# Transforms in two tiles, their products issued in two groups, and k moved ahead of the taps, in a two-layer convolution kernel

## The chip, the cores and the metric

The kernel runs on one core of a Trainium2 chip. A core has five engines with queues of their own: TensorE (PE) for matrix products, VectorE (DVE) and ScalarE (ACT) for elementwise work, GpSimd (POOL), and SyncE (SP), which here issues all transfers. An engine works its queue in order; between engines, instructions wait on semaphores. TensorE reads SBUF and writes PSUM, the accumulator memory; VectorE and ScalarE read both. The metric is the device time of one launch in microseconds (us). Before the change three timed runs gave 3358.13, 3359.34 and 3363.5 us, median 3359.34.

## The reference

x is (4, 64, 256, 256) in float32. Two layers, each with a residual:

```
x = x + L0(gn(x));  x = x + L1(gn(x))        # gn: group norm, 32 groups of 2 channels
L0: h = gelu(conv3x3(x, c1));  h = c2 * h    # 1x1, 64 -> 128 channels
    xa, k = split(h)
    xs = gelu(vertical3(horizontal3(xa)))    # depthwise
    gate = top 2 of 3 of softmax(mean(xs) @ gate_w)
    out = xs + sum_i gate_i * w3_i((w2_i k) * (w1_i xs));  L0 = proj * out
L1: h = relu(bn(conv3x3(x, quantized w1)));  relu(bn(conv3x3(h, quantized w2)) + x)
```

Batch norm (bn) needs statistics over all four images, so layer 1 is cut into two passes and a last elementwise pass.

## The kernel before, in words

**Stages.** First comes layer 0 for the images b = 0 to 3, called the front here (about 57 to 1530 us of the profiled execution), interleaved with the statistics of the next image and with the second half of layer 0 (the expert output, `plan_out`) of the image before. Then come the first convolution of layer 1, its second convolution, and the last pass, which TensorE has no part in. The change touches the front alone.

**The front.** An image is worked in 32 octets (n = 0 to 31) of 8 rows, one per step; step g = 32 b + n. The 3x3 convolution uses a transform along the row: for every pair of neighbouring pixels POOL forms four combinations of the inputs, the products 0 to 3 (`front_v`, L479 to L487), and TensorE multiplies each with a weight of its own. The weights of products 0 and 3 are `c1s`, those of 1 and 2 are `u12`, with a factor 0.5 in them (L419). All combinations lie in one SBUF tile, `v_ring`, with 12 slots, that is three octets of 4 slots each. One call of `front_v` makes half an octet: 4 POOL instructions of 128x256 elements, products 1, 2, then 0, 3.

**Accumulation.** An octet accumulates in a PSUM buffer `ps_c`, of which there are two. Products 1 and 2 come first (`front_conv_a` and then `front_conv_b` with (1, 2)). Then ACT and DVE turn their sums into a butterfly in place (`front_butterfly`, L553 to L555), and one step later products 0 and 3 are added on top (the same functions with (0, 3)). ACT then writes h with two gelu instructions (`front_h`, L561). The next octet but one uses the same buffer.

**The rest of a step.** `front_taps_a` and `front_taps_b` (L597, L602) apply the 1x1 and vertical taps to h, into the single buffer `ps_a`. `front_taps_h` (L606 to L628) evicts it: ACT L610, DVE L611, L614 and L617, ACT L628. `front_proj` (L648) projects. Once in four steps, at step 32 b + 4 j + 5, `front_k` (L630) makes the ranks of k out of four octets of h: 16 matmul calls, 32 passes on the array, and an eviction by ACT, L646. `front_q` does the like for xs. `front_k`, `front_q`, `front_proj`, `out_slot` (L741, the expert output of the image before, evicted by DVE L757) and all small products share one PSUM buffer, called "p".

**What sets the order.** `at(step, order, call)` (L157) puts a call on a plan, and the plan is recorded sorted by (step, order). The engines' queues are that order, except that ACT is ordered by the framework's scheduler until step 124 (L1006). The orders of one step are:

| order | call | engine |
|---|---|---|
| 0 | `front_pad`, `front_load` | POOL, SP |
| 0.5 | `front_k` | PE, ACT |
| 1 | `front_conv_a` (1, 2) of octet g | PE |
| 2 | `out_slot` | PE, DVE |
| 3 | `front_conv_a` (0, 3) of octet g-1 | PE |
| 4 | `front_taps_a` of octet g-3 | PE |
| 5 | `divide` | POOL |
| 5.6 | layer 1's preparations, last steps only | ACT, POOL |
| 6 | `front_proj` | PE, DVE |
| 7 to 8.5 | `front_conv_b` (1, 2), butterfly, `front_conv_b` (0, 3), `front_h` | PE, ACT, DVE |
| 9, 9.5 | `front_v` of half 1 of octet g+1, of half 0 of octet g+2; `front_taps_b` | POOL; PE |
| 10, 11 | `front_q`; `front_taps_h` | PE, DVE; ACT, DVE |

`divide` (L435) is a one-element POOL memset, the tick: it waits for the matmuls of orders 1 to 4, and the `front_conv_b` matmuls wait for it.

**The start.** Before step 0 the statistics of image 0 end in `stats_end(0)` (L391): it scales the weights (L405), forms `u12` (L411 to L413), the sum `both` (L415 to L417), halves `u12` (L419), and multiplies `both` with the mean for the bias `c1_bias` of the gelu (L422, L424).

Of the kernel before, what the change touches and what calls it, by code (L numbers as in the profile page):

```python
# [9 lines left out]
F32 = mybir.dt.float32  # L10
F32R = mybir.dt.float32r
AF = mybir.ActivationFunctionType
ALU = mybir.AluOpType
# [4 lines left out]
B, C, H, W = 4, 64, 256, 256  # L18
P = 128
# [44 lines left out]
def conv_preact_kernel(ctx: ExitStack, tc: tile.TileContext, io, col128, colset, col64):  # L64
    nc = tc.nc
# [15 lines left out]
    def small(name):  # L81

        return bank("p", name)[:, 0, 0, :]
# [64 lines left out]
    front = ExitStack()  # L148
    front_pool = front.enter_context(tc.tile_pool(name="front", bufs=1, reuse_waits="tile"))

    VSLOTS = 12
    v_ring = front_pool.tile([P, VSLOTS, 4, W // 2], F32, name="v_ring")


    plan = defaultdict(list)
# [1 line left out]
    def at(step, order, call, *args):  # L157
        plan[step, order].append((call, args))
# [12 lines left out]
    def c128(name):  # L171
        return m128[:, col128[name][0] : col128[name][1]]
# [120 lines left out]
    def group_norm(st, avg, out, name):  # L293
        mv = stat.tile([P, 1, 2], F32, tag="mv", name=f"mv_{name}")
        nc.vector.bn_aggr(mv[:, 0, :], flat(st))
        yield
        yield from combine(mv, 1, avg, eps, out, name)
# [71 lines left out]
    gn1, gn2, c1s, u12, v_edge, c1_bias = {}, {}, {}, {}, {}, {}  # L369
# [21 lines left out]
    def stats_end(b):  # L391


        own = stat.tile([P, 2], F32, tag="gx", name=f"gx_{b}")
        yield from group_norm(st_x.pop(b), c128("avgx"), own, f"x{b}")
        yield
        gn1[b] = stat.tile([P, 2], F32, tag="gn1", name=f"gn1_{b}")
        v_edge[b] = lstat.tile([P, W // 2], F32, tag="v_edge", name=f"v_edge_{b}")
        ps = small(f"ps_gx_{b}")
        nc.tensor.matmul(ps[:, 0:2], c128("from_x"), own, start=True, stop=True)  # L400
        nc.vector.tensor_copy(gn1[b], ps[:, 0:2])
        c1s[b] = lstat.tile([P, 3, 3, C], F32, tag="c1s", name=f"c1s_{b}")

        engine = nc.gpsimd if b else nc.vector
        engine.tensor_scalar(  # L405
            c1s[b].rearrange("p a b c -> p (a b c)"), c128("c1"), gn1[b][:, 1:2], None, ALU.mult
        )
        engine.tensor_scalar(v_edge[b], zeros[:, 0 : W // 2], gn1[b][:, 0:1], 2.0, ALU.add, ALU.mult)
        u12[b] = lstat.tile([P, 3, 2, C], F32, tag="u12", name=f"u12_{b}")
        ends = lstat.tile([P, 3, C], F32, tag="u_ends", name=f"u_ends_{b}", bufs=1)  # L410
        engine.tensor_tensor(ends, c1s[b][:, :, 0, :], c1s[b][:, :, 2, :], ALU.add)  # L411
        for i, op in enumerate((ALU.add, ALU.subtract)):
            engine.tensor_tensor(u12[b][:, :, i, :], ends, c1s[b][:, :, 1, :], op)  # L413

        engine.tensor_tensor(ends[:, 0, :], u12[b][:, 0, 0, :], u12[b][:, 1, 0, :], ALU.add)  # L415
        for half in (slice(0, C), slice(C, P)):
            engine.tensor_tensor(both[half, half], ends[half, 0, :], u12[b][half, 2, 0, :], ALU.add)  # L417
        u = u12[b].rearrange("p a b c -> p (a b c)")
        engine.tensor_scalar(u, u, 0.5, None, ALU.mult)  # L419
        yield  # L420
        ps = small(f"ps_cb_{b}")
        nc.tensor.matmul(ps[:, 0:1], both, gn1[b][:, 0:1], start=True, stop=True)  # L422
        c1_bias[b] = stat.tile([P, 1], F32, tag="c1b", name=f"c1b_{b}")
        nc.vector.tensor_tensor(c1_bias[b], c128("c1_b"), ps[:, 0:1], ALU.subtract)  # L424


    xs_of, hs, xss, k_sb, pooled, open_c, open_a = {}, {}, {}, {}, {}, {}, {}
# [48 lines left out]
    def v_slot(b, n, slot):  # L476
        return (4 * (b * NOCT + n) + slot) % VSLOTS

    def front_v(b, n, half, products=((1, 2), (0, 3))):  # L479

        x = xs_of[b, n // 2]
        i = 4 * (n % 2) + 2 * half
        d = [x[:, i : i + 2, q : q + W - 1 : 2] for q in range(4)]
        terms = {0: (d[0], d[2], ALU.subtract), 1: (d[1], d[2], ALU.add), 2: (d[2], d[1], ALU.subtract), 3: (d[3], d[1], ALU.subtract)}
        o = v_slot(b, n, 2 * half)
        for p in (p for ps in products for p in ps):
            nc.gpsimd.tensor_tensor(v_ring[:, o : o + 2, p, :], *terms[p])  # L487

    def conv_tile(b, n, t, in_half, products, first, last):


        ps = open_c[b, n][:, t].rearrange("p a b -> p (a b)").rearrange("p (e q c) -> p e q c", e=2, q=GP)
        terms = {
            (0, 0): ([(1, 0), (2, 1)], [(0, 0), (1, 1)]),
            (0, 1): ([(0, -2)], [(2, 1)]),
            (1, 0): ([(0, 1)], [(2, 2)]),
            (1, 1): ([(1, 1), (2, 0)], [(0, 1), (1, 0)]),
        }[t, in_half]

        def pieces(slot, p):  # L500

            a, e = (v_slot(b, n, s) for s in (slot, slot + 2))
            before, after = slot < 0 and n == 0, slot + 2 > 3 and n == NOCT - 1
            if not before and not after and e == a + 2:
                return [(v_ring[:, a : e + 1 : 2, p, :], (0, 2))]
            two = []
            for q, at_v, outside in ((0, a, before), (1, e, after)):
                if not outside:
                    two.append((v_ring[:, at_v : at_v + 1, p, :], (q, q + 1)))
                elif p == 1:  # L510
                    two.append((v_edge[b].unsqueeze(1), (q, q + 1)))
            return two

        lists = []
        for out_half in range(2):
            calls = []
            for p in products:
                for ky, slot in terms[out_half]:
                    w = c1s[b][:, ky, p // 3 * 2, :] if p in (0, 3) else u12[b][:, ky, p - 1, :]

                    calls += [(ps[:, p // 2, :, :], w, rhs, to) for rhs, to in pieces(slot, p)]
            lists.append(
                [
                    (
                        (ps_e, out_half, in_half, w, rhs, to),
                        dict(start=(first and i == 0), stop=(last and i == len(calls) - 1), skip_group_check=True),
                    )
                    for i, (ps_e, w, rhs, to) in enumerate(calls)
                ]
            )  # L530
        return lists
# [343 lines left out]
    first_v = ((0, 0), (0, 1), (1, 0))  # L875
    for n, half in first_v:
        front_v(0, n, half, ((1, 2),))
    for _ in stats_end(0):
        pass
    for k in range(2):  # L880
        front_pad(0, k)
    for n, half in first_v:
        front_v(0, n, half, ((0, 3),))

    def at_each(places, chain):

        for place in places:
            at(*place, next, chain, None)
# [8 lines left out]
    def plan_front(b):  # L897
        t = b * F_STEPS
        place = tail if b == B - 1 else (lambda step: step)
        for k in range(NCH):  # L900
            if b > 0 or k >= 2:
                for call in (front_alloc, front_pad, front_load):
                    at(max(t + 2 * k - 3, 0), 0, call, b, k)
        for n in range(NOCT):
            g = t + n
            at(g, 1, front_conv_a, b, n, (1, 2))
            at(place(g + 1), 3, front_conv_a, b, n, (0, 3))
            at(place(g + 3), 4, front_taps_a, b, n)
            at(g, 5, divide)
            for step in (g + 1, g + 3):  # L910
                if step >= CONV1:
                    at(place(step), 5, divide)
            at(place(g + 4), 6, front_proj, b, n)
            at(g, 7, front_conv_b, b, n, (1, 2))
            at(g, 7.5, front_butterfly, b, n)
            at(place(g + 1), 8, front_conv_b, b, n, (0, 3))
            at(place(g + 1), 8.5, front_h, b, n)
            if b > 0 or n > 0:
                at(g - 1, 9, front_v, b, n, 1)
            if b > 0 or n > 1:  # L920
                at(g - 2, 9.5, front_v, b, n, 0)
            at(place(g + 3), 9, front_taps_b, b, n)
            at(place(g + 3), 11, front_taps_h, b, n)
        for j in range(NOCT // 4):
            at(place(t + 4 * j + 5), 0.5, front_k, b, j)
            at(place(t + 4 * j + 7), 10, front_q, b, j)
        e = place(t + NOCT + 3)
        at_each(((e, 2.5), (e, 5.7), (e, 8.7)) if e < CONV1 else ((e + 1, 12.7), (e + 3, 12.7), (e + 5, 12.7)), gate(b))
# [60 lines left out]
    for b in range(B):  # L989
        plan_front(b)  # L990
        if b < B - 1:
            plan_stats(b + 1, b * F_STEPS + 1, 2.7)
            t = (b + 1) * F_STEPS + 4
            e = t + NOCT + 1
# [6 lines left out]
        else:  # L1001
            t, e = CONV1 + 36, CONV1 + b * (NG + 1) - 10
# [93 lines left out]
    with tc.manual_schedule(  # L1096
# [15 lines left out]
        for d in range(2 * len(chunks)):  # L1112
            i = d // 2
# [35 lines left out]
    for i, (b, k) in enumerate(steps):  # L1149
# [10 lines left out]
        j = i - 3 + KEEP  # L1160
# [115 lines left out]
```

## Time and profile before

| | |
|---|---|
| median of three runs | 3359.34 us |
| the profiled execution | 3359.5 us, its span 3357.7 us |
| PE | 2682.6 us busy, 80% |
| VectorE, ScalarE, GpSimd | 2680.4, 1659.6 and 1610.8 us busy |
| granted TensorE clock | mean 0.914; 1.00 from 60 to 1462 us |

A time on the profile is that of one profiled execution, counted from the start of its span; 1.8 us of its own time lie outside the span. In a line of the timeline the columns are start, duration, engine, line, operation, output and inputs, count, and in brackets the idle time of the engine before it with the instruction that ended it. Consecutive instructions of the same kind are merged. "PEld" is TensorE's weight load. The releaser in brackets is inferred: where an instruction waits for several semaphores it is one of them.

### The profile page before, as it was taken

Reading aid. Unit: us, or ns where it says so; the run is one execution under the profiler, and the core shown is the slowest. Engines: PE = TensorE matmul, PEld = TensorE weight load, DVE = VectorE, ACT = ScalarE, POOL = GpSimd, SP = SyncE. Lnnn points to the kernel's source line nnn. Section 1 sums busy time; section 2 is a strip of 40 time slices with the busy share of each in tenths; the row PEclk is TensorE's granted clock in tenths of the full one; section 3 lists DMA queues with packets and bytes.
Section 4 is the critical chain, followed back from the end, with each engine's and each line's share of the span. In section 5 each row is a group of like instructions: output and inputs, shape, how many; then the busy total and the mean of one; then the engine's idle time right before and its main releaser. Section 6 shows DMA issues by size and latency. Waiting matters only on the chain.

```text
span 3357.7 us, 60548 instructions
## 1 busy us (share of the span) xinstructions
PE 2682.6 (80%) x24832; PEld 1776.4 (53%) x24832; DVE 2680.4 (80%) x2810; ACT 1659.6 (49%) x1799; POOL 1610.8 (48%) x1833
## 2 busy tenths in 40 slices
PE   2999999999999999987899999999999999300000
PEld 1555555554555555544667777777877878200000
DVE  7666588878888777765899998988999999866666
ACT  0344444344444444334566666767777777322222
POOL 2444544443444444443678777757777777100000
PEclk9999999999999999988899999999999999655555
DMA  8665688878887767764688887665666664599999
GB/s 304 173 180 127 160 257 276 245 206 274 264 257 217 212 195 208 201 187 142 243 280 295 310 288 243 222 247 184 236 232 233 237 236 172 207 412 412 412 412 386
DMA packets 356453, 838.27 MB, mean 250 GB/s; under 512 B 22288, under 2 KB 284944, under 8 KB 293456
## 3 DMA queue, kind: packets, MB, share of 16 engines
q1 hardware_dynamic: 356176, 834.40, 74.5%
q8 instruction: 195, 3.19, 0.4%
q14 instruction: 82, 0.67, 0.1%
HBM read 493.00 MB, written 341.31 MB: 248 GB/s over the span
## 4 chain that ended last, share of the span: by engine, by line
PE 67%; DVE 11%; DMA 11%; issue 3%; ACT 2%; POOL 2%; SPq 2%; ACTq 0%; POOLq 0%; DVEq 0%
PE ps_h L305 24%; PE ps_c L444 19%; DMA y_end<-y_d 10%; PE ps_a L444 8%; PE ps_o L749 3%; PE ps_h2m L305 3%; PE ps_p L444 3%; PE ps_hm L305 2%; DVE half L351 2%; PE ps_k L638 2%; PE ps_q L676 2%; DVE h L331 2%; POOL v_ring L487 1%; DVE st_x L389 1%; SPq L1163 1%
## 5 line engine op out<-in xcount | busy, mean ns | idle before, releaser
L305 PE MATMUL ps_h<-half,w_q 128*128 128x512 f32 x4096 | 1034.1, 404 | 22.7 <-DVE h L331 16.1
L305 PEld LDWEIGHTS ps_h<-half,w_q 128*128 128x128 f32 x4096 | 778.8, 191 | 252.4 <-issue 25.9
L487 POOL TENSOR_TENSOR v_ring<-x 128x256 f32<-128x256 f32 x1024 | 596.8, 616 | 161.8 <-PE ps_c L444 115.1
L367 POOL TENSOR_TENSOR sum<-s,sum 128x640 fp32r<-128x640 f32 (+1 forms) x256 | 556.9, 2196 | 195.0 <-ACT sum L365 189.3
L444 PE MATMUL ps_c<-v_ring,u 64*64 64x256 f32 (+1 forms) x6472 | 390.1, 372 | 52.6 <-POOL v_ring L487 43.7
L444 PEld LDWEIGHTS ps_c<-v_ring,u 64*64 64x64 f32 x6472 | 266.4, 134 | 266.5 <-POOL v_ring L487 142.5
L331 DVE SCALAR_TENSOR_TENSOR h<-ps_h,scale_w,m 128x1024 f32<-128x1024 f32 x256 | 326.9, 1277 | 90.3 <-ACT m L330 90.2
L444 PE MATMUL ps_a<-h,av 64*64 64x512 f32 (+1 forms) x3568 | 385.5, 533 | 10.4 <-DVE t L614 9.1
L444 PE MATMUL ps_c<-v_ring,c1s 64*64 64x256 f32 (+1 forms) x6472 | 390.6, 371 | 0.5 <-DVE ps_c L555 0.5
L437 POOL MEMSET tick<- 128x1 f32 x132 | 13.1, 99 | 696.8 <-PE ps_a L444 688.9
L444 PEld LDWEIGHTS ps_c<-v_ring,c1s 64*64 64x64 f32 x6472 | 267.1, 134 | 133.5 <-DVE t L611 29.6
L628 ACT ACTIVATE xs<-t 128x1024 f32<-128x1024 f32 x128 | 135.4, 1058 | 371.8 <-DVE t L617 333.6
L553 ACT ACTIVATE m<-ps_c 128x512 f32<-128x512 f32 x128 | 76.6, 599 | 442.8 <-PE ps_c L444 437.4
L1154 ACT ACTIVATE v<-y_end,shift,gn 128x2048 f32<-128x2048 f32 x64 | 133.8, 2092 | 321.6 <-DMA y_end<-y_d 314.8
L1155 DVE SCALAR_TENSOR_TENSOR h<-h,ss,v 128x2048 f32<-128x2048 f32 x64 | 150.2, 2350 | 160.8 <-ACT v L1154 158.0
L611 DVE SCALAR_TENSOR_TENSOR t<-ps_a,m,t 128x1020 f32<-128x1020 f32 x128 | 163.5, 1278 | 122.8 <-ACT t L610 122.8
L351 DVE TENSOR_TENSOR half<-h,half 128x1280 fp32r<-128x1280 f32 (+1 forms) x128 | 254.4, 2029 | 7.7 <-ACT half L349 7.7
L662 DVE TENSOR_TENSOR x<-ps_p,x 128x1024 f32<-128x1024 f32 x128 | 156.2, 1220 | 120.7 <-PE ps_p L444 97.2
L444 PEld LDWEIGHTS ps_a<-h,av 64*64 64x64 f32 x3568 | 165.6, 134 | 127.2 <-issue 94.1
L351 DVE TENSOR_TENSOR half<-yn,half 128x1280 fp32r<-128x1280 f32 x80 | 210.4, 2646 | 4.2 <-ACT half L349 4.2
L330 ACT ACTIVATE m<-ps_hm,m,scale_w 128x512 f32<-128x512 f32 x128 | 99.6, 778 | 225.3 <-PE ps_hm L305 197.1
L561 ACT ACTIVATE h<-ps_c,c1b 128x512 f32<-128x512 f32 x256 | 174.1, 739 | 38.8 <-PE ps_c L444 38.8
(186 smaller groups left out, 4097.3 us busy)
## 6 DMA issues: line engine op xcount, KB each, us to landing
h_d<-h SPq DMA_DIRECT2D x117, 1024.0 KB, 4.8
h<-h_d SPq DMA_DIRECT2D x64, 1152.0 KB, 7.1
yn<-y_d SPq DMA_DIRECT2D x60, 1152.0 KB, 7.7
xs_in<-in_x SPq DMA_DIRECT2D x64, 1024.0 KB, 8.9
x<-in_x SPq DMA_DIRECT2D x256, 256.0 KB, 4.9
y<-t_d SPq DMA_DIRECT2D x64, 1024.0 KB, 8.4
y_d<-y SPq DMA_DIRECT2D x256, 256.0 KB, 5.3
y_end<-y_d SPq DMA_DIRECT2D x64, 1024.0 KB, 11.3
```

Of the source, the lines that this page charges most:

```text
L305: nc.tensor.matmul(ps[:, 0 : n * HW], w[:, k, m, :], t[:, i + m : i + m + n, c : c + HW], start=(j == 0), stop=(j == len(terms) - 1),)
L331: nc.vector.scalar_tensor_tensor(h.rearrange("p a (b e) -> p e (a b)", e=2), by_two(ps)[:, :, 0 : n * HW], w_scale[w], m.unsqueeze(1).to_b ...
L351: engine.tensor_tensor(lower, y, upper.bitcast(F32), ALU.subtract)
L367: nc.gpsimd.tensor_tensor(tiles[1][:, a:e, :], t, tiles[0][:, a:e, :].bitcast(F32), ALU.subtract)
L444: last[:] = [nc.tensor.matmul(ps[o, at_out[0] : at_out[1], :], w[i], rhs[i], **flags)]
L487: nc.gpsimd.tensor_tensor(v_ring[:, o : o + 2, p, :], *terms[p])
L561: nc.scalar.activation(h.rearrange("p q (c e) -> p e q c", e=2), c[:, t].rearrange("p (e q c) -> p e q c", e=2, q=GP), AF.Gelu, bias=c1_bi ...
L611: nc.vector.scalar_tensor_tensor(t[:, :, 1:W], ps[:, :, 0 : W - 1], sh[:, 0:1], t[:, :, 1:W], ALU.mult, ALU.add)
L628: nc.scalar.activation(flat(xss[b, n]), flat(t), AF.Gelu, accum_out=pooled[b][:, n : n + 1])
L662: nc.vector.tensor_tensor(t1, ps, t1, ALU.add)
L1154: nc.scalar.activation(v, y, AF.Identity, bias=shift[:, b : b + 1], scale=gn2[b][:, 1:2])
L1155: nc.vector.scalar_tensor_tensor(h, h, ss2[:, 0:1], v, ALU.mult, ALU.add)
```

## The change

The combinations go into two tiles, one for products 1 and 2 and one for products 0 and 3. For every octet, products 1 and 2 of both halves are made at order 5.4, right behind the tick, and products 0 and 3 at 9 and 9.5, as all four were before. `front_k` moves from order 0.5 to 3.5, behind both `front_conv_a` and in front of `front_taps_a`. In `stats_end` the halving of `u12` comes ahead of `both`, and the bias takes the factor -2 in return; for image 0 the product that makes the bias is recorded behind the first `front_conv_a` (order 1.5 of step 0).

```diff
-    v_ring = front_pool.tile([P, VSLOTS, 4, W // 2], F32, name="v_ring")
+    v_rings = [front_pool.tile([P, VSLOTS, 2, W // 2], F32, name=f"v_ring{i}") for i in range(2)]
+    def v_of(p):
+        return v_rings[p in (0, 3)][:, :, p // 2, :]
...
+        u = u12[b].rearrange("p a b c -> p (a b c)")
+        engine.tensor_scalar(u, u, 0.5, None, ALU.mult)
         engine.tensor_tensor(ends[:, 0, :], u12[b][:, 0, 0, :], u12[b][:, 1, 0, :], ALU.add)
         for half in (slice(0, C), slice(C, P)):
             engine.tensor_tensor(both[half, half], ends[half, 0, :], u12[b][half, 2, 0, :], ALU.add)
-        u = u12[b].rearrange("p a b c -> p (a b c)")
-        engine.tensor_scalar(u, u, 0.5, None, ALU.mult)
         yield
...
-        nc.vector.tensor_tensor(c1_bias[b], c128("c1_b"), ps[:, 0:1], ALU.subtract)
+        nc.vector.scalar_tensor_tensor(c1_bias[b], ps[:, 0:1], -2.0, c128("c1_b"), ALU.mult, ALU.add)
...
-            nc.gpsimd.tensor_tensor(v_ring[:, o : o + 2, p, :], *terms[p])
+            nc.gpsimd.tensor_tensor(v_of(p)[:, o : o + 2, :], *terms[p])
...
-    for _ in stats_end(0):
-        pass
+    first_end = stats_end(0)
+    for _ in range(5):
+        next(first_end)
+    at(0, 1.5, next, first_end, None)
...
-            if b > 0 or n > 0:
-                at(g - 1, 9, front_v, b, n, 1)
-            if b > 0 or n > 1:
-                at(g - 2, 9.5, front_v, b, n, 0)
+            for half, before in ((1, 1), (0, 2)):
+                if b > 0 or n > before - 1:
+                    at(g - before, 5.4, front_v, b, n, half, ((1, 2),))
+                    at(g - before, 9 if half else 9.5, front_v, b, n, half, ((0, 3),))
...
-            at(place(t + 4 * j + 5), 0.5, front_k, b, j)
+            at(place(t + 4 * j + 5), 3.5, front_k, b, j)
```

More of the change, by code (lines that the diff above doesn't have):

```diff
@@ L504, in pieces @@
             if not before and not after and e == a + 2:
-                return [(v_ring[:, a : e + 1 : 2, p, :], (0, 2))]
+                return [(v_of(p)[:, a : e + 1 : 2, :], (0, 2))]
             two = []
@@ L508, in pieces @@
                 if not outside:
-                    two.append((v_ring[:, at_v : at_v + 1, p, :], (q, q + 1)))
+                    two.append((v_of(p)[:, at_v : at_v + 1, :], (q, q + 1)))
                 elif p == 1:
```

## The prediction

> **What bounds the kernel now.** I read the page first, for the stage that the change touches.
>
> ```profile
> PE   2999999999999999987899999999999999300000
> PEclk9999999999999999988899999999999999655555
> L487 POOL TENSOR_TENSOR v_ring<-x 128x256 f32<-128x256 f32 x1024 | 596.8, 616 | 161.8 <-PE ps_c L444 115.1
> ```
>
> The first two rows are PE's busy tenths and its granted clock in 40 slices of 84 us. The front, slices 1 to 18, is PE at 90% or more with an undisturbed clock. POOL's transforms are long, but what counts is who waits for them. The table of waits seems to say TensorE does (total us, times, longest):
>
> ```profile
> PEld ps_c L444 <- POOL v_ring L487: 142.5, 121, 6.5
> PE ps_c L444 <- POOL v_ring L487: 43.7, 53, 5.6
> POOL tick L437 <- PE ps_a L444: 688.9, 125, 12.4
> ```
>
> The timeline of a step with no k and no q corrects that:
>
> ```profile
> 875.90 1.19 POOL L487 TENSOR_TENSOR v_ring<-x 128x256 f32<-128x256 f32 x2
> 878.07 1.04 PE L444 MATMUL ps_a<-h,av 64*64 64x512 f32 x8
> 878.38 1.34 ACT L561 ACTIVATE h<-ps_c,c1b 128x512 f32<-128x512 f32 x2 [0.33 <-PE ps_c L444]
> 879.82 1.96 PE L444 MATMUL ps_c<-v_ring,u 64*64 64x256 f32 x32 [0.71 <-POOL v_ring L487]
> 881.71 1.13 PE L749 MATMUL ps_o<-ranks,wm 32*128 32x512 f32 x4
> 882.76 1.96 PE L444 MATMUL ps_c<-v_ring,c1s 64*64 64x256 f32 x32
> 883.65 1.28 DVE L757 SCALAR_TENSOR_TENSOR y<-ps_o,ob,y 128x1024 f32<-128x1024 f32 x1
> 884.54 1.04 PE L444 MATMUL ps_a<-h,av 64*64 64x512 f32 x8
> ```
>
> The matmul at 879.82 opens octet g. In the compiled program it waits for two things: the first two POOL instructions behind the tick (products 1 and 2 of its half 1), done at 877.09, and the second gelu of octet g-2, which frees the PSUM buffer, done at 879.72. So the 0.71 us are ACT's, not POOL's. In each of the 53 steps of this sort between 90 and 1465 us the matmul starts 0.10 us after the gelu's end. Now a step with k:
>
> ```profile
> 866.08 1.04 PE L444 MATMUL ps_a<-h,av 64*64 64x512 f32 x8
> 866.41 1.38 ACT L561 ACTIVATE h<-ps_c,c1b 128x512 f32<-128x512 f32 x2 [0.31 <-PE ps_c L444]
> 867.05 2.06 PE L638 MATMUL ps_k<-h,wk 64*32 64x512 f32 x32
> 869.04 1.96 PE L444 MATMUL ps_c<-v_ring,u 64*64 64x256 f32 x32
> 871.99 1.96 PE L444 MATMUL ps_c<-v_ring,c1s 64*64 64x256 f32 x32
> 873.77 1.90 PE L444 MATMUL ps_a<-h,av 64*64 64x512 f32 x18
> ```
>
> Here the gelu ends at 867.79, but PE works on k until 869.1 and there is no gap. k stands in the hole that the gelu leaves; q, at order 10, does the same two steps later.
>
> **The Trainium skill.** *PSUM — Partial Sum Buffer*, "The four PSUM rules", says GpSimd cannot touch PSUM, so POOL cannot be what frees a PSUM buffer; the trace agrees in that the gap follows ACT. *Perfetto Trace Analysis*, "Per-instruction lifecycle", says the propagation of a semaphore lies outside the profiled window; the 0.10 us is that here. *TensorE: Matmul & The Clock Gate*, "Part 1", says PE drops to half clock after about 3.4 us idle; the trace has it after 3.00 us (below), and not after 0.7. *GPSIMD Engine Reference*, "Specifications", has POOL contend with DVE instructions that have two SBUF inputs. The front's large DVE work has PSUM or one input, and L662 takes 1.21 to 1.23 us with or without POOL beside it.
>
> **The change, part by part.**
>
> *Transforms.* 1024 instructions of 0.616 us before and after. Behind the tick POOL ran 2, waited for PE (0.83 us), ran 6; now it runs 4, waits at most briefly for the same matmuls of `front_conv_b` (0, 3), and runs 4, about 1 us sooner done. Behind them stand the pads and the next tick, and the tick finds POOL idle for 5.5 us on average (688.9/125). PE's one early need, the two products at 877.09, comes as early as before. Two tiles remove orderings that PE didn't wait for. I cost it at 0; it is bounded at a gain of 0.7 us a step by the gap if I misread that (rival A). DVE's and SP's queues keep their order; k and the bias issue no transfers (k's store belongs to `front_q`).
>
> *One place gains.* In step 126 layer 1's first preparation stands at 5.6, between tick and transforms:
>
> ```profile
> 1489.24 3.08 POOL L359 TENSOR_TENSOR s<-yn 128x640 f32<-128x640 f32 x2
> 1498.03 3.69 PE L444 MATMUL ps_c<-v_ring,u 64*64 64x256 f32 x32 [5.63 <-POOL v_ring L487]
> ```
>
> There products 1 and 2 really are late, first done at 1497.97. Now they go first, but L359 and what ACT makes from it (L365, ahead of L553 and the gelu in ACT's queue) come 1.2 us later, so the gelu ends at 1494.69+1.2 = 1495.9 and the matmul starts about 1496.0: -2.0. If the shorter hole also spares the half clock (3.69 against 1.96), up to -4.5.
>
> *k at 3.5.* 32 times. From the start of `front_taps_b` (866.08, 878.07) to that of the next `front_taps_a`:
>
> Without `out_slot` (8 steps, b = 0), k steps take 6.45 now. Afterwards, as in plain steps, the second `front_conv_a` starts at 3.51; 1.89 until another PSUM bank follows (879.82 to 881.71); k to its successor 1.95: 7.35. +0.90 each, +7.2.
>
> With it (22 steps) 7.66 now. Afterwards the second `front_conv_a` starts at 4.69 and k could start at 6.58. But k needs buffer "p", which `out_slot` has just filled. Its eviction L757 stands behind L611, L614 and L617 on DVE and ends at 6.86 in the step above (884.93-878.07). k starts 0.1 later, 6.98 with the k steps' own L617 (0.02 later): +1.95 = 8.93, so +1.27 each, +27.9. Behind k on PE are the taps, the projection and all that follows. ACT's L646 now follows L628, and the projection waits for it: k ends at 8.95, L646 takes 1.11, 10.2 against a projection at 8.93+1.72 = 10.65. Hidden with 0.45 to spare; if not, +0.45 a step.
>
> The k of step 125 is different, because ACT is in plan order there and L646 stood behind L628, with `out_slot` waiting:
>
> ```profile
> 1470.55 2.08 PE L749 MATMUL ps_o<-ranks,wm 32*128 32x512 f32 x4 [3.00 <-ACT k L646]
> 1472.56 3.69 PE L444 MATMUL ps_c<-v_ring,c1s 64*64 64x256 f32 x32
> ```
>
> That step takes 13.37 (1462.66 to 1476.03). With k behind `out_slot` the wait and the half clock go and it takes 8.93: -4.4. The last k (step 130) has no `front_conv_a` to pass: 0.
>
> *The bias.* Now the first matmul starts at 67.56, behind L415 and L417 (0.52 + 1.11 us), L419 (0.67), L422 and L424. Afterwards L419 follows L413 (ended 65.00) and the matmul starts near 65.8: -1.75. L422 (0.59 on PE) then stands between the two halves of octet 0; the tick's wait (0.24) hides part, so -1.5. For the other images L415 to L419 swap on POOL, and L424 keeps one 0.15 us instruction: 0.
>
> Sum: 7.2 + 27.9 - 4.4 - 2.0 - 1.5 = +27.2. All of it lies on PE's queue in a stage where PE is the path, and layer 1 follows. Against the profiled execution: 3359.5 + 27.2 = 3386.7; that execution lies 0.2 above the median, so 3387 either way. Differences under 0.2% (6.7 us) can't be told from none.
>
> **Rivals.**
>
> A. POOL is the releaser after all, as the table of waits says. Then the early products close the hole in plain and k steps: -43.7 (the row "PE ps_c"), -1.5, and k's move costs only its wait for "p" (0.4 x 22 = 9): 3323 us, faster. It decides if the second transform behind the tick ends after the gelu; in the trace it ends 2.6 us before. 6%.
>
> B. k doesn't wait for "p", because DVE gets to L757 earlier: +0.90 in 30 steps, 27.0 - 7.9 = +19: 3378. Against it: DVE's order is unchanged in the compiled program, and L757 begins right at L617's end. 16%.
>
> C. The projection waits for L646 as well, 0.45 x 30 = +13: 3400. Against it the 0.45 us to spare. 10%.
>
> D. No measurable change: k covers a wait at the taps instead of the gelu's. Plain steps with no `out_slot` do wait there 0.25 us, and steps behind q 0.41, but k steps don't. It would need 0.9 us. 6%.
>
> **How the numbers follow.** The forecast's own chance is 62%, as 3387 with about 3380 to 3393 around it: the "p" wait within 0.2 us (4), the junction's -2.0 to -4.5, the start's -1.75 to 0. A range of 3372 to 3398 takes in B and part of C and leaves out A, D and the rest of C. Faster 6% (A), same 6% (D), slower 88%.
>
> **What would show it.** In the profile after: k steps with a gap of 0.7 us ahead of the matmul on u, 0.10 us behind the gelu; k behind the second `front_conv_a`, 0.1 us after L757's end where there is an `out_slot`; plain steps at 10.7 us as before and the same gap in them, with POOL done earlier; the 3.00 us wait at the step-125 `out_slot` gone; the first matmul near 65.8. Wrong would be: gaps gone in plain steps (A), k without its wait (B), a gap at `ps_p` in k steps (C).

## The result and the profile after

The changed kernel takes 3378.58 us (median of five runs, 3375.86 to 3380.8) against 3359.34 (3357.76 to 3363.5): a ratio of 1.0055, 95% interval 1.004 to 1.007. It is slower by 19.2 us, where 27.2 were forecast. Its profiled execution took 3377.74 us with a span of 3376.0, 18.3 more than before. Lines that were L487, L444, L561, L757 and L638 are now L492, L449, L566, L762 and L643, five further down.

The page of the changed kernel, PE's busy tenths, its granted clock and the row of the transforms:

```profile
PE   2999999999999999997899999998999999300000
PEclk9999999999999999998999999999999999755555
L492 POOL TENSOR_TENSOR v_ring<-x 128x256 f32<-128x256 f32 x1024 | 593.3, 617 | 61.4 <-DMA x<-in_x 47.2
```

POOL's transforms take what they took (593.3 against 596.8 us) and hardly wait for TensorE any more: the row's idle time fell from 161.8 to 61.4 us, of which 47.2 are one wait for a transfer. That nothing came of this on TensorE is seen in the table of waits of the changed kernel (total us, times, longest):

```profile
POOL tick L442 <- PE ps_a L449: 811.2, 127, 11.2
PEld ps_c L449 <- POOL v_ring L492: 157.9, 124, 3.0
PE ps_c L449 <- POOL v_ring L492: 63.4, 91, 2.6
PE ps_k L643 <- DVE y L762: 3.5, 22, 0.2
```

POOL is done earlier in every step and waits longer at its tick (811.2 against 688.9 us), and yet more of TensorE's idle time is put down to it: 63.4 us in 91 waits, 43.7 in 53 before. Where an instruction waits for several semaphores, the table names one. The last row is new: k waits for buffer "p" 22 times.

A step of the changed kernel with k and `out_slot`, in its timeline:

```profile
882.03 1.34 ACT L566 ACTIVATE h<-ps_c,c1b 128x512 f32<-128x512 f32 x2 [0.32 <-PE ps_c L449]
883.46 1.96 PE L449 MATMUL ps_c<-v_ring,u 64*64 64x256 f32 x32 [0.73 <-POOL v_ring L492]
885.35 1.13 PE L754 MATMUL ps_o<-ranks,wm 32*128 32x512 f32 x4
886.41 1.96 PE L449 MATMUL ps_c<-v_ring,c1s 64*64 64x256 f32 x32
887.11 0.17 DVE L622 TENSOR_TENSOR t<-t,ends 128x8 f32<-128x8 f32 x1
887.19 1.28 DVE L762 SCALAR_TENSOR_TENSOR y<-ps_o,ob,y 128x1024 f32<-128x1024 f32 x1
888.52 1.95 PE L643 MATMUL ps_k<-h,wk 64*32 64x512 f32 x32 [0.16 <-DVE y L762]
```

The gelu ends at 883.37 and the matmul on u starts at 883.46 behind a gap of 0.73 us, which k filled before. k starts at 888.52, 0.05 us behind the end of L762. In the next step of the same timeline, one without k, the gap is the old one, although the transforms now run in one piece:

```profile
892.59 4.62 POOL L492 TENSOR_TENSOR v_ring<-x 128x256 f32<-128x256 f32 x8
895.07 1.35 ACT L566 ACTIVATE h<-ps_c,c1b 128x512 f32<-128x512 f32 x2 [0.33 <-PE ps_c L449]
896.52 1.96 PE L449 MATMUL ps_c<-v_ring,u 64*64 64x256 f32 x32 [0.72 <-POOL v_ring L492]
```

Steps 125 and 126 of the changed kernel:

```profile
1495.05 1.13 PE L754 MATMUL ps_o<-ranks,wm 32*128 32x512 f32 x4
1496.11 1.96 PE L449 MATMUL ps_c<-v_ring,c1s 64*64 64x256 f32 x32
1498.23 1.95 PE L643 MATMUL ps_k<-h,wk 64*32 64x512 f32 x32 [0.16 <-DVE y L762]
1519.77 3.38 PE L449 MATMUL ps_c<-v_ring,u 64*64 64x256 f32 x32 [3.53 <-POOL half L356]
1524.14 1.96 PE L449 MATMUL ps_c<-v_ring,c1s 64*64 64x256 f32 x32
```

The 3.00 us wait of step 125 and its half clock are gone, and the gap of step 126 fell from 5.63 to 3.53 us. (32 passes of the convolution take 1.96 us at full clock; where they take up to 3.7 us, TensorE was at half clock for some or all of them.)

Set against each other octet by octet (start of the first matmul on u of each octet, after minus before), the two traces give this account of the 18.3 us:

| where | forecast | the two traces |
|---|---|---|
| k without `out_slot`, 8 steps | 8 x 0.90 = +7.2 | 8 x 0.83 = +6.6 |
| k with `out_slot`, 22 steps | 22 x 1.27 = +27.9 | 22 x 1.07 = +23.5 |
| step 125 | -4.4 | -4.9 |
| plain steps | 0 | 0 (each within 0.03) |
| step 126: gap; half clock | -2.0; 0 to -2.5 | -2.1; -3.0 |
| start up to octet 2; half clock in octet 2 | -1.5; not named | +0.1; +1.7 |
| steps with the gate's chain | 0 | -1.5, and -1.7 of half clock |
| layer 1 and the rest | 0 | -0.4 |
| sum | +27.2 | +18.3 |

The start of the changed kernel's trace lies 0.6 us late before the change has any part in it: `ps_gx` starts at 62.39 against 61.80. The parts named half clock belong to this pair of executions and not to the change alone: other executions with the same order of work at that place have them or lack them (last section).

### The profile page after: what moved, and what is told of

Read it like the earlier page. It is cut to its first block, busy times and chain, and to the rows that moved or that the text cites. A ratio compares the mean times of both kernels' runs of the same rounds, so it can differ in the third digit from the quotient of the medians.

```text
span 3376.0 us, 60519 instructions
## 1 busy us (share of the span) xinstructions
PE 2683.1 (79%) x24832; PEld 1772.7 (53%) x24832; DVE 2679.1 (79%) x2810; ACT 1658.2 (49%) x1799; POOL 1606.3 (48%) x1833
## 4 chain that ended last, share of the span: by engine, by line
PE 58%; DVE 14%; DMA 12%; POOL 7%; issue 4%; ACT 4%; SPq 3%; POOLq 0%; ACTq 0%; DVEq 0%
PE ps_h L310 23%; PE ps_c L449 14%; DMA y_end<-y_d 10%; PE ps_a L449 7%; POOL v_ring L492 5%; PE ps_h2m L310 3%; PE ps_o L754 3%; PE ps_hm L310 2%; PE ps_p L449 2%; DVE half L356 2%; PE ps_k L643 2%; PE ps_q L681 2%; DVE h L336 2%; DVE y L762 1%; DVE t L619 1%
## 5 line engine op out<-in xcount | busy, mean ns | idle before, releaser
L492 POOL TENSOR_TENSOR v_ring<-x 128x256 f32<-128x256 f32 x1024 | 593.3, 617 | 61.4 <-DMA x<-in_x 47.2
L449 PE MATMUL ps_c<-v_ring,u 64*64 64x256 f32 (+1 forms) x6472 | 391.3, 372 | 74.9 <-POOL v_ring L492 63.4
L449 PEld LDWEIGHTS ps_c<-v_ring,u 64*64 64x64 f32 x6472 | 273.6, 134 | 283.2 <-POOL v_ring L492 157.9
L442 POOL MEMSET tick<- 128x1 f32 x132 | 13.1, 99 | 820.1 <-PE ps_a L449 811.2
L449 PE MATMUL ps_a<-h,av 64*64 64x512 f32 (+1 forms) x3568 | 386.3, 534 | 10.4 <-DVE t L619 9.1
L449 PE MATMUL ps_c<-v_ring,c1s 64*64 64x256 f32 (+1 forms) x6472 | 387.3, 368 | 0.5 <-DVE ps_c L560 0.5
L449 PEld LDWEIGHTS ps_c<-v_ring,c1s 64*64 64x64 f32 x6472 | 267.9, 133 | 129.0 <-DVE t L616 47.8
L616 DVE SCALAR_TENSOR_TENSOR t<-ps_a,m,t 128x1020 f32<-128x1020 f32 x128 | 163.5, 1277 | 122.2 <-ACT t L615 122.2
L449 PEld LDWEIGHTS ps_a<-h,av 64*64 64x64 f32 x3568 | 161.9, 133 | 148.5 <-issue 112.5
L566 ACT ACTIVATE h<-ps_c,c1b 128x512 f32<-128x512 f32 x256 | 172.2, 731 | 38.8 <-PE ps_c L449 38.8
```

The costliest lines, as they stand in the source:

```text
L449: last[:] = [nc.tensor.matmul(ps[o, at_out[0] : at_out[1], :], w[i], rhs[i], **flags)]
L492: nc.gpsimd.tensor_tensor(v_of(p)[:, o : o + 2, :], *terms[p])
L566: nc.scalar.activation(h.rearrange("p q (c e) -> p e q c", e=2), c[:, t].rearrange("p (e q c) -> p e q c", e=2, q=GP), AF.Gelu, bias=c1_bi ...
L616: nc.vector.scalar_tensor_tensor(t[:, :, 1:W], ps[:, :, 0 : W - 1], sh[:, 0:1], t[:, :, 1:W], ALU.mult, ALU.add)
```

## The experiments

**Each part alone.** k alone, the bias alone, the transforms alone, and the whole change with k put back.

k alone, in the kernel before:

```diff
-            at(place(t + 4 * j + 5), 0.5, front_k, b, j)
+            at(place(t + 4 * j + 5), 3.5, front_k, b, j)
```

> The kernel before with k alone moved, from order 0.5 to 3.5. Theory G (the hole ahead of the products 1 and 2 belongs to ACT's gelu, and k used to stand in it): 8 steps without out_slot at +0.83, 22 with out_slot at +1.06, step 125 -4.9, as the trace of the changed kernel has them: 6.6 + 23.3 - 4.9 = +25, so about 3384, slower than the full change. Step 126 keeps a gap near 5.6 us. Rival P (POOL's transforms own the hole, and the early products gave back part of what k lost everywhere): k alone costs clearly more, +35 or above. Rival O (k is innocent, the loss comes from the split or the start): within 3 us of the kernel before.

Measured: 3386.85 us, 26.3 above the kernel before on the same chip (3360.51), ratio 1.008 (95% interval 1.0067 to 1.0094). The gap ahead of the matmuls on u in k steps went from none to 0.70 us (median of its trace), and step 126 kept 5.63. More than the whole loss is k's.

The bias alone: the halving of `u12` ahead of `both`, the factor -2, and the bias's matmul at order 1.5 of step 0, as in the change's diff.

> The kernel before with the change of the bias alone. Theory G: the first matmul comes about 1.7 us sooner after the mean is known, the bias's own matmul and the tick take most of that back, so -0.5 us for octet 0; whether TensorE falls to half clock in octet 2 decides another 0 or +1.7. Between -2 and +2, not measurable: 3357 to 3361. The prediction had -1.5. Rival O: +5 or more, if the start is what made the changed kernel slower.

Measured: 3358.21 us, ratio 0.9995 (0.9986 to 1.0003): not to be told from no change. Its timeline shows why the start is worth less than 1.5 us:

```profile
65.79 3.69 PE L445 MATMUL ps_c<-v_ring,u 64*64 64x256 f32 x32 [3.46 <-DVE u L416]
69.41 0.58 PE L423 MATMUL ps_cb<-gn,both 128*128 128x1 f32 x2
73.74 1.96 PE L445 MATMUL ps_c<-v_ring,c1s 64*64 64x256 f32 x32 [0.48 <-DVE ps_c L556]
80.49 2.99 PE L445 MATMUL ps_c<-v_ring,u 64*64 64x256 f32 x32 [2.59 <-POOL v_ring L488]
```

The first matmul comes 1.77 us sooner (67.56 before), but octet 0's products 0 and 3 only 0.65 (74.39 before). TensorE takes 3.69 us instead of 3.30 for the first 32 passes, and the bias's matmul of 0.58 us stands in between. (The 3.69 are not the new start's alone: `k_only`, with the old one, took 3.67.) Then octet 2 is at half clock, 2.99 us instead of 1.96, behind a hole that is not longer than before (2.59, 2.58).

The transforms alone: two tiles, and orders 5.4, 9 and 9.5.

> The kernel before with the transforms alone changed: two tiles, products 1 and 2 at 5.4, products 0 and 3 at 9 and 9.5. Theory G: nothing in the plain steps, their gap stays 0.7 us and starts 0.10 us behind the gelu; step 126 gains 2.1 us of gap and 3 us of half clock, the steps with the gate about 0.7 each for DVE working without POOL beside it: -5 to -8, about 3352. Rival P: the gap closes in plain steps and the kernel is 30 to 45 us faster, 3315 to 3330. Rival O: slower than before.

Measured: 3354.11 us, ratio 0.9982 (0.9974 to 0.9989), 6.4 us faster. The gap of plain steps keeps its median of 0.69 us, and step 126 has the shorter one, in the timeline of this kernel:

```profile
1486.27 2.09 POOL L491 TENSOR_TENSOR v_ring<-x 128x256 f32<-128x256 f32 x2
1488.33 2.24 POOL L364 TENSOR_TENSOR s<-yn 128x640 f32<-128x640 f32 x2
1493.03 2.69 PE L448 MATMUL ps_c<-v_ring,u 64*64 64x256 f32 x32 [3.54 <-POOL half L356]
```

As much again comes from the three steps where the gate is computed on DVE (-0.7, -0.7 and -0.7 us net in this trace). What is left of the 6.4 us is not pinned down; this trace also has 1.2 us less of half clock in step 125, which the transforms have no part in (`bias_only` has the same). In the kernel before, the timeline of the first of the three steps has the gate's small instructions beside POOL:

```profile
435.17 2.90 POOL L487 TENSOR_TENSOR v_ring<-x 128x256 f32<-128x256 f32 x5 [0.24 <-PE ps_c L444]
436.42 0.53 DVE L710 TENSOR_TENSOR beat<-gate 128x3 f32<-128x3 f32 x1
436.98 0.55 DVE L711 TENSOR_SCALAR beat<-beat 128x3 f32<-128x3 f32 x1
437.56 0.67 DVE L714 TENSOR_TENSOR keep<-beat 128x1 f32<-128x1 f32 x3
```

and with the transforms alone changed, POOL ends at 437.43 and the second and third are short:

```profile
435.67 1.76 POOL L491 TENSOR_TENSOR v_ring<-x 128x256 f32<-128x256 f32 x3 [0.24 <-PE ps_c L448]
436.92 0.53 DVE L714 TENSOR_TENSOR beat<-gate 128x3 f32<-128x3 f32 x1
437.48 0.17 DVE L715 TENSOR_SCALAR beat<-beat 128x3 f32<-128x3 f32 x1
437.68 0.30 DVE L718 TENSOR_TENSOR keep<-beat 128x1 f32<-128x1 f32 x3
```

The changed kernel with k at 0.5:

> The changed kernel with k back at order 0.5. Theory G: the 30 steps lose their second gap, step 125 gets its 3.00 us wait and half clock back: 25 us below the changed kernel, about 3353, and some 6 us faster than before. Rival P: k hides POOL's wait in these steps, so the same sign but at most 10 us below the changed kernel. Rival O: no faster than the changed kernel.

Measured: 3351.78 us, ratio 0.9975 (0.9968 to 0.9983): 8.7 us faster than before, and 26.8 below the changed kernel. The parts add up within their intervals: 26.3 - 2.3 - 6.4 = 17.6, against 19.2 for all three together.

**Whose hole is it?** The table of waits names POOL. So POOL was made late, in two doses, in the kernel with k at 0.5 (`range(2)`, and `range(6)` for the second):

```diff
+    def delay():
+        for _ in range(2):
+            nc.gpsimd.tensor_tensor(zeros[:, 0:W], zeros[:, 0:W], zeros[:, 0:W], ALU.add)
...
             at(g, 5, divide)
+            at(g, 5.2, delay)
```

> The changed kernel with k at order 0.5, and behind every tick two more POOL instructions of 128x256 (they add zeros to zeros), so that all transforms of a step come about 1.2 us later. Theory G (ACT's gelu owns the hole of 0.7 us in plain steps; the second transform behind the tick ends 2.6 us before the gelu): 1.4 us are still to spare, no plain step gets longer, the gap stays 0.7 us and 0.10 us behind the gelu; only step 126, where POOL is the late one, loses about 1.2 us: within 3 us of the kernel with k back at 0.5, which had 3351.8. Rival P (POOL owns it): 1.2 us in each of 53 plain steps, +60 us, 3410 or more.

> The same with six such instructions, 3.7 us. Theory G: now the second transform ends about 1.1 us behind the gelu, so POOL does become the late one: about +1.1 us in each plain step, and little in k and q steps, where 2 us of other work stand ahead of these matmuls: +50 to +70 us over the kernel with k at 0.5, 3400 to 3420. Rival P: three times the loss of two instructions, near +190, 3540.

Measured: 3352.24 us with two (ratio to the kernel before 0.9977, 0.9971 to 0.9984), 0.5 from the kernel without them; 3414.03 us with six (1.0169, 1.0155 to 1.0183), 62 above. The timeline with two:

```profile
877.16 4.63 POOL L496 TENSOR_TENSOR v_ring<-x 128x256 f32<-128x256 f32 x8
878.44 1.35 ACT L570 ACTIVATE h<-ps_c,c1b 128x512 f32<-128x512 f32 x2 [0.33 <-PE ps_c L453]
879.89 1.96 PE L453 MATMUL ps_c<-v_ring,u 64*64 64x256 f32 x32 [0.72 <-POOL v_ring L496]
```

and with six:

```profile
911.70 1.33 ACT L570 ACTIVATE h<-ps_c,c1b 128x512 f32<-128x512 f32 x2 [0.33 <-PE ps_c L453]
913.18 4.62 POOL L496 TENSOR_TENSOR v_ring<-x 128x256 f32<-128x256 f32 x8
913.85 1.96 PE L453 MATMUL ps_c<-v_ring,u 64*64 64x256 f32 x32 [1.42 <-POOL v_ring L496]
```

The bracket is the same in both and true in the second only. With two, all transforms come 1.3 us later and the matmul starts 0.10 us behind the gelu, as ever. With six the gelu ends at 913.03 and the matmul waits until 913.85, when the first transform of 0.62 us is done: it needed that one alone, not two as the forecast had it. (The kernel before has the same in step 126: its matmul of 1498.03 follows the first transform, done at 1497.97, and not the second, done at 1498.55.) So the gap grew by 0.7 us a plain step, not 1.1. Against the trace without the delay, which is 63.6 us shorter, 45 steps grew by 0.5 to 1.0 us each, 33 us in sum; 10 us more arise between the first matmul and octet 4, and the rest in single steps of up to 3.7 us, most of them near the borders of images. With nothing added, the first transform ends 3.2 us ahead of the gelu (893.21 against 896.42 in the step above), and making it earlier can't gain.

**Step 125 alone keeps the moved k:**

```diff
-            at(place(t + 4 * j + 5), 0.5, front_k, b, j)
+            at(place(t + 4 * j + 5), 3.5 if (b, j) == (B - 1, 6) else 0.5, front_k, b, j)
```

> The changed kernel with k at order 0.5 in every step but 125, where it stays at 3.5. Theory G: the moved k is worth 4.9 us there and nothing anywhere else, so about 3347, some 13 us below the kernel before. Rival: what step 125 gains is lost again at the 3.5 us gap of step 126, so 3352 as with k at 0.5 throughout.

Measured: 3349.85 us, ratio 0.9973 (0.9963 to 0.9983). That is 1.9 us below k at 0.5 throughout, and the two intervals overlap: the times alone don't show a gain. The traces do, and a smaller one than 4.9: step 125 gains 3.7 us against the trace of `k_back`. The other 1.2 are a half clock that lasted 6.8 us there in the kernel before, and 3.4 us in `bias_only`, `v_only`, `k_back` and `pool_late_2`, all with k at 0.5 and a wait of 2.98 to 3.00 us. (In step 67 the trace of `k_back_but_125` loses 3.0 us to half clock, which step 125 has no part in.)

**Other work in the hole.** If the hole is the gelu's, any matmuls that need neither its result nor its PSUM buffer can stand there. In the last kernel, `out_slot` goes to the steps' gap where neither k nor q fills it:

```diff
-                at(steps[2 * k + i], order, out_slot, b, k, i)
+                s = steps[2 * k + i]
+                at(s, 0.6 if s < CONV1 and s % 4 > 1 else order, out_slot, b, k, i)
```

> The same, and out_slot at order 0.6 instead of 2 in the steps that hold neither k nor the matmuls behind q (46 of them, images 1 to 3). Theory G: any work of TensorE put into the gelu's hole gains the hole: the second front_conv_a comes 0.70 us sooner, the taps, the projection and buffer p have 0.4 us or more to spare: 46 x 0.65 = -30 against the kernel without it, about 3317. Rival V (DVE, about 9.5 us busy in a step of 10.7, becomes the bound): half of that, about 3332. Rival P: the hole moves behind out_slot and nothing is gained, 3347.

Measured: 3323.61 us, ratio 0.9896 (0.9881 to 0.9911), 26.2 below the kernel without it. The timeline:

```profile
867.67 1.35 ACT L566 ACTIVATE h<-ps_c,c1b 128x512 f32<-128x512 f32 x2 [0.33 <-PE ps_c L449]
868.34 1.13 PE L754 MATMUL ps_o<-ranks,wm 32*128 32x512 f32 x4
869.39 1.96 PE L449 MATMUL ps_c<-v_ring,u 64*64 64x256 f32 x32
871.17 1.91 PE L449 MATMUL ps_c<-v_ring,c1s 64*64 64x256 f32 x32
```

The gap is gone; TensorE passes from the taps to `out_slot` and from there to u without a pause.

**Buffer "p" in the k steps.** In the changed kernel, `out_slot` goes to 0.6 in the steps that hold k (`s % 4 == 1` in the same two lines).

> The changed kernel, k at 3.5, with out_slot at order 0.6 instead of 2 in the steps that hold k (images 1 to 3, 22 of them). Theory G with the rule of buffer p: out_slot fills the gelu's hole and the second front_conv_a comes 0.70 us sooner, but k can't start before VectorE's L762 has emptied p, and that stands behind L616, L619 and L622, which don't move: k starts when it did, its wait grows from 0.16 to about 0.86 us, and nothing is gained, 3376 to 3381. Rival F (k is bound by TensorE's queue alone): 22 x 0.65 = -14, about 3364.

Measured: 3377.3 us, ratio 1.0056 (1.0043 to 1.0069), the changed kernel's own 1.0055. The timeline of the same step as above:

```profile
884.04 1.13 PE L754 MATMUL ps_o<-ranks,wm 32*128 32x512 f32 x4
885.10 1.96 PE L449 MATMUL ps_c<-v_ring,u 64*64 64x256 f32 x32
886.87 1.91 PE L449 MATMUL ps_c<-v_ring,c1s 64*64 64x256 f32 x32
888.56 1.28 DVE L762 SCALAR_TENSOR_TENSOR y<-ps_o,ob,y 128x1024 f32<-128x1024 f32 x1
889.89 1.95 PE L643 MATMUL ps_k<-h,wk 64*32 64x512 f32 x32 [1.11 <-DVE y L762]
```

The hole is filled and k waits 1.11 us instead of 0.16. From the gelu's start to k's it is 6.49 us in both (889.89-883.40, 888.52-882.03). What sets k is DVE's chain L616, L619, L622, L762 behind the gelu; with k at 3.5 and this order on DVE, filling TensorE's hole does not shorten the step.

**The hole in image 0**, which has no `out_slot`: there the projection of the step before goes into it.

```diff
-            at(place(g + 4), 6, front_proj, b, n)
+            s = place(g + 4)
+            at(*((s + 1, 0.6) if b == 0 and s < F_STEPS and s % 4 in (1, 2) else (s, 6)), front_proj, b, n)
```

> The kernel with k back at 0.5 except in step 125 and out_slot at 0.6 (3323.6), and in image 0, where there is no out_slot, the projection of the step before in the hole of the steps that hold neither k nor the matmuls behind q: front_proj from (s, 6) to (s + 1, 0.6) for 15 steps. Theory G: it gains the hole of 0.70 us there too, but the step before is the one that loses the projection, so what is bound there by the taps' evictions may keep part: -5 to -10, about 3316. Rival V (DVE or the taps' buffer is next in image 0): no gain, 3324.

Measured: 3314.67 us, ratio 0.9873 (0.9856 to 0.989), against 0.9896 for `fill_out`, whose interval overlaps this one. Its trace gains 0.28 us in each of these steps, not 0.70; there are 14 of them, not 15, so that 4 us are shown by the trace, and the rest of the 8.9 between the medians is not. The timeline shows what took the rest:

```profile
207.60 1.09 PE L449 MATMUL ps_c<-v_ring,u 64*64 64x256 f32 x20 [0.33 <-POOL tick L442]
210.24 1.04 PE L449 MATMUL ps_p<-xs,m 64*64 64x512 f32 x8
211.12 1.96 PE L449 MATMUL ps_c<-v_ring,u 64*64 64x256 f32 x32
```

The gap ahead of u (211.12) is gone. But the projection had stood between the taps and the matmuls that wait for the tick (207.60), and without it that wait lies bare, 0.33 us. By its median this is the fastest of the kernels, 1.3% below the kernel before.

## Why the prediction was right

The sign, the mechanism and the place were right, the size 8 us too high. In the two traces it is 8.9: k cost 5.0 us less than forecast, the steps with the gate 3.2 less, steps 125 and 126 3.6 less and the rest 0.4 less, and the start cost 3.3 more. The parts named half clock, which differ between executions, make up 3.0 of this, net; that part is luck, good or bad. By its own steps:

- *Transforms at 0 in the plain steps.* Right, and shown from both sides: earlier transforms gained nothing there, and transforms 1.3 us later lost nothing. Rival A is dead. That the matmul waits for "the first two POOL instructions behind the tick" was wrong in detail; one is enough.
- *k without `out_slot`, +0.90.* Measured +0.83: the taps follow k's start by 1.88 us (median), not by 1.95.
- *k with `out_slot`, +1.27.* This is the largest mis-sized term: measured +1.07, 4.4 us in 22 steps. The wait for "p" exists, but its length was read from a step of another sort. `out_slot` comes in two forms, s = 0 and s = 1. The step at 878.07 holds s = 0, where L757 starts 3.83 us behind the matmul on u and ends at 5.12. The k steps hold s = 1; the kernel before has L757 from 3.73 to 5.01 (median) in the other steps with s = 1, and the changed kernel has the same in its k steps. (Whether the form itself makes the 0.1 us isn't shown.) And k followed L762 by 0.05 us, not 0.1, and the taps followed k by 1.88, not 1.95: 0.10 + 0.05 + 0.07 is the 0.2 that is missing. The time came out at rival B's number, but not by rival B: k does wait for "p", and `fill_k` shows that this wait decides the step.
- *Step 125, -4.4.* The trace has -4.9, but 1.2 of that are a longer half clock that the kernel before had in this one execution; against `k_back` the moved k gains 3.7. The forecast took the single trace's half clock for the kernel's own.
- *Step 126, -2.0, up to -4.5 with the half clock.* The gap lost 2.1. The half clock there lost 3.0 between these two traces, but this is not the shorter hole's doing alone: `k_only`, with the old hole of 5.63 us, took 3.69 us for the matmul on u and then 1.96 for the next 32 passes, while `v_only`, with 3.54, took 2.69 and then 3.55.
- *The bias, -1.5.* Wrong. The first matmul moved by the 1.75 us that were forecast, but 0.65 us were left at octet 0's products 0 and 3: the bias's own 0.58 us weren't hidden, and the first 32 passes took 0.39 us longer than in the one trace of the kernel before. The changed kernel's +1.7 in octet 2 is no effect of the change: the hole is 2.58 to 2.60 us in the kernel before, in the changed one and in the first four experiments, and 32 passes behind it took 1.96, 2.81, 3.49, 2.99, 1.96 and 3.52 us. The third of these, at half clock, has the old start, and `pool_late_2`, with the new one, was at full clock.
- *Nothing for the gate's steps.* Missed: -1.5 us in the two traces, DVE's small instructions beside POOL. The other -1.7 there are a half clock in step 35 that the changed kernel's execution did not have; `fill_k`, with the same transforms and k, has it again and takes 1.7 us more in this step than the changed kernel. So it is no gain of the change, and that it cancels the +1.7 in octet 2 is luck.
- *Rival C* fell: the projection follows the taps without a gap in k steps (890.40 + 1.95 overlaps 892.18). *Rival D* fell by the interval.

Why one and the same hole of 2.6 us costs half clock in one execution and not in another is worked out in the last section. It matters here because the prediction read the half clock of steps 125 and 126 from a single execution.

## What to carry to other kernels

A hole of a few tenths in TensorE's queue belongs to whoever releases it last, and a bracket in the profile names only one of several; compare the end times of all releasers, and make one of them late if in doubt. Work that stood in such a hole was free here, and moving it elsewhere cost the hole plus whatever buffer it met there; filling a hole gains less than its length where the moved work had itself hidden a wait (0.28 of 0.70 us for the projection). Before filling a hole, look for the next chain through a shared buffer: the same `out_slot` in the same hole gained 26 us in 46 steps and nothing in those where k waits for "p". A half clock read from one execution is not yet a property of the kernel.

## What the runs showed of the hardware that was not expected

Small DVE instructions were held until POOL's current transform ended. On 3 elements per partition they took 0.53 and 0.55 us while POOL ran transforms (L710 and L711 of the kernel before), and their like in the changed kernel, at 444.19 and 444.38 with POOL idle, 0.16 and 0.17. In the kernel before they end at 436.95 and 437.53, within 0.03 us of the ends of POOL's third and fourth transforms (436.93 and 437.50). In `v_only`, whose POOL stops at 437.43, the first ends at 437.45 and the second takes 0.17. L707, on 9 elements, ends 0.03 us behind a transform in the kernel before (436.38, 436.35), in `v_only` (436.88, 436.85) and in the changed kernel (444.15, 444.12), and takes 0.57, 0.57 and 0.45 us. Two others in the same stretch, L705 and L706, took 0.15 and 0.17 us beside POOL and were not held. L710 has two SBUF inputs, L707 and L711 have one, and scalars. The row that the prediction draws on (the Trainium skill, *GPSIMD Engine Reference*, "Specifications") names a second case that the prediction left out, DVE instructions in a 2-port perf mode; no run here shows whether L707 and L711 are in one.

Behind the hole ahead of octet 2, 2.6 us in all of them, TensorE was at reduced clock in nine of the twelve profiled executions and at full clock in three (the kernel before, `v_only`, `pool_late_2`). The traces' record of the granted clock shows why. Within an execution all changes of the clock lie on one grid of 3.41 us, and every stretch at half clock is a whole number of such windows long (the last of a trace is cut by its end); where the grid lies differs between executions. Two windows around octet 2 of the kernel before, and two of the changed one (the stretch, its length and TensorE's busy time come first; the third number from the end is the clock):

```profile
77.15:80.57 3.42, 1.46 (x28) 0.81 (x20) 2.04 (x4) 2.68 (x4) 3.42 (x8) 1.00 0.96 217
80.57:83.98 3.41, 2.79 (x52) 2.42 (x56) 1.13 (x2) 0.52 (x1) 0.60 (x2) 1.00 1.10 282
78.88:82.29 3.41, 0.96 (x20) 0.85 (x24) 2.91 (x5) 2.34 (x3) 2.42 (x5) 1.00 1.19 223
82.29:85.71 3.42, 3.42 (x40) 2.58 (x36) 0.00 (x0) 0.00 (x0) 0.00 (x0) 0.50 0.97 381
```

In the kernel before, a border of the grid cuts the hole, so that TensorE is idle for 1.96 us of one window, and the next stays at full clock. In the changed kernel nearly all of the hole lies in one window, 2.45 us are idle, and the next is at half clock. Over the twelve executions, between 75 and 1530 us, a window at full clock was followed by half clock in 41 of 41 cases where TensorE was idle for more than 2.0 us of it, in 15 of 38 with 1.5 to 2.0 us, and in none of 4961 with less. The idle time need not be in one piece: in step 35 of the kernel before, where the clock halves at 432.14, the 1.76 us in the window ahead come from two waits with 0.39 us of work between them. So the prediction's 3.00 us were not the shortest wait with half clock behind it in that trace, and the 1.00 given there for the clock from 60 to 1462 us is a rounded mean. Why the band between 1.5 and 2.0 us goes both ways stays open.
